# Attention on Trainium2: the softmax reciprocals turned in 32x32 blocks on VectorE and spread over partitions by DMA, with the out-projection two units later

## The chip, the cores and the metric

The kernel runs on one core of one Trainium2 chip. The core has five engines, each with its own queue of instructions that it works through in order: TensorE (PE in the profile, PEld for its weight loads), VectorE (DVE), ScalarE (ACT), GpSimd (POOL) and SyncE (SP), which here only issues transfers. An instruction that waits for a semaphore holds up everything behind it on its own queue. Matrix products write PSUM, which has eight banks of 512 float32 columns on 128 partitions; everything else lives in SBUF (128 partitions) or in device memory, and DMA engines move it between the two.

The metric is the device time in microseconds of one execution, as the median of several runs. A profiled execution is one of its own, so its time stands beside its span.

## The reference

Four layers run one after the other on x of shape 64 x 64 x 256 (64 sequences of 64 tokens), with a conditioning vector of 64 numbers for each sequence. The change lies in the second one:

```python
def _attention(x, W_q, W_k, W_v, W_o):          # 16 heads of 16
    q, k, v = split(x @ W_q.T), split(x @ W_k.T), split(x @ W_v.T)
    attn = softmax(scale * einsum('bnqd,bnkd->bnqk', q, k), axis=-1)
    o = einsum('bnqk,bnkd->bnqd', attn, v)
    return o.transpose(0, 2, 1, 3).reshape(b, l, dm) @ W_o.T

x = x + a_alpha * _attention(_ada_rmsnorm(x, ...), W_q, W_k, W_v, W_o)
return x + f_alpha * _swiglu(_ada_rmsnorm(x, ...), gate_w, hidden_w, out_w, out_b)
```

The first layer is a gated feed-forward network with quantised activations, the third a layer norm, the fourth an adapter whose weights depend on the conditioning.

## The kernel before

The 4096 tokens are worked in 8 blocks of 512 tokens (8 sequences). The first layer runs from 0 to about 258 us, the attention from there to about 445 us, and the feed-forward network of the second layer with the rest from there to the end.

The attention is a loop over 16 units (`for w in range(W)`, line 1070). Unit w is half a block: 4 sequences, 256 tokens. `i, tp = divmod(w, 2)` gives the block and the half; "even" and "odd" units below are tp 0 and 1. Inside a unit the work is split in the steps that the helper functions name:

- `a_score` (649): 64 small products of q and k into four PSUM banks, tag S, of which there is one set.
- `a_shift` (660, 662): for each half of the scores, e = 0 and 1, VectorE takes the maximum of each row and subtracts it; the result is `ex` in SBUF.
- `a_exp` (667, ScalarE) and `a_sum` (671, VectorE): the exponential, and its sum over the keys.
- `a_recip` (676, VectorE): `rz`, the reciprocals of the sums, 32 for each of the 128 partitions. A partition is a query here.
- `a_turn` (690 to 694): 16 transposes on TensorE turn `ex`, so that the keys lie on the partitions; four copies bring them from PSUM to SBUF as `pts`. In odd units two of the four are VectorE's, the other two and all of those of even units ScalarE's.
- `a_weigh` (709): 64 small products of `pts` with the values into one PSUM bank, `po`. Here the partitions are (head, feature), and the columns are queries.
- `a_parts` (725, 726): `of`, the attention's output, is split into a high and a low part, `oh` and `ol`, on ScalarE and POOL. All large products here are three passes over such parts.
- `a_project` (741, 742): the out-projection on TensorE, a product with `at` (from `load_rows`) on VectorE, and an addition on POOL; after odd units the block is stored to memory.

The reciprocals lie on the wrong side for `po`: in `rz` a query is a partition, in `po` it is a column. Before, `a_rows` (681) has ScalarE spread `rz` to `rp`, each reciprocal 16 times side by side, and `a_weigh` turns `rp` with four TensorE transposes (716) into a PSUM bank, copies `po` to SBUF as `of` on ScalarE (713) and multiplies the two on VectorE (717).

The loop is skewed: in unit w the weighing, the parts and the projection of unit w-1 are done. Beside this, each unit does three groups of products for the next block (`todo`: values at lines 83 to 85 through `a_val`, queries and keys through `a_qk`), the norm turns of the block after that (`a_norm_turn`: four TensorE transposes, 259 on VectorE, 260 on POOL, and then its split on ScalarE and POOL), and a splitting of weights for the feed-forward network (`splits.turn`, lines 214 to 219): ScalarE casts (217) a staging tile `st`, POOL subtracts (218), and SP loads the next one (211). There are two staging tiles. One is loaded before the loop; units 1 to 13 call `turn` once, and units 4, 8 and 12 call it twice. The queries, keys and values of the last two units are done, so these hold products of the feed-forward network instead (`f_keep`).

In PSUM, four banks hold S, and four (tag mm) are handed round among `po`, the `todo` products, the norm turns, the out-projection and the transposes of `a_turn`.

What sets the order: the kernel's own text. `tc.manual_schedule(engines=...)` keeps the instructions of the named engines in the order in which the code issues them. In the attention these are TensorE, ScalarE, VectorE and POOL. SP is not named, so its transfers are ordered by the scheduler: `vb` (line 615, the values laid out for the weighing, four transfers per block), `rows` (271), the blocks `ax` (584) and the weight loads (211).

Of the kernel before, what the change touches and what calls it, by code (L numbers as in the profile page):

```python
# [8 lines left out]
F32 = mybir.dt.float32  # L9
# [3 lines left out]
ALU = mybir.AluOpType  # L13
# [4 lines left out]
P = 128  # L18
# [18 lines left out]
def tile_kernel(ctx: ExitStack, tc, xT, x, condT, cw, upT, downT, qkvT, woT, ghT, outT_w,  # L37
# [9 lines left out]
    alphad = dram.tile([3, NB, D], F32, name="alphad")  # L47
    s1d = dram.tile([2, NB, 128, BN], F32, name="s1d")
    s2d = dram.tile([2, NB, 64, D], F32, name="s2d")


    pools = {}
# [9 lines left out]
    def bank(tag):  # L62
        uid[0] += 1
        tags = pools["tags"]
        if tag not in tags:
            tag = "mm"
        return pools["ps"].tile([P, 512], F32, tag=tag, bufs=tags[tag], name=f"{tag}_{uid[0]}")
# [587 lines left out]
    def a_shift(w, e):  # L655

        pool, U = pools["b"], units[w]
        sv = U["pS"][:, 2 * e:2 * e + 2].rearrange("p j (a l) -> p (j a) l", l=L)
        ms = U["mx"][:, 0, 16 * e:16 * e + 16]
        nc.vector.tensor_reduce(ms, sv, AX.X, ALU.max)  # L660
        ex = pool.tile([P, 16, L], F32, tag="ex2", bufs=2, name=f"ex{w}_{e}")
        nc.vector.tensor_tensor(ex, sv, ms.unsqueeze(2).broadcast_to([P, 16, L]), ALU.subtract)
        U["ex"].append(ex)

    def a_exp(w, e):
        ex = units[w]["ex"][e]
        nc.scalar.activation(ex, ex, AF.Exp, scale=0.25)

    def a_sum(w, e):
        pool, U = pools["b"], units[w]  # L670
        nc.vector.tensor_reduce(U["mx"][:, 1, 16 * e:16 * e + 16], U["ex"][e], AX.X, ALU.add)

    def a_recip(w):
        pool, U = pools["b"], units[w]
        rz = U["rz"] = pool.tile([P, 4, 4, 2], F32, tag="rz", bufs=2, name=f"rz{w}")
        nc.vector.reciprocal(rz, U["mx"][:, 1].rearrange("p (j a h) -> p a j h", j=4, h=2))

    def a_rows(w):

        rp = units[w]["rp"] = pools["b"].tile([P, 32, 16], F32, tag="rp", bufs=1, name=f"rp{w}")  # L680
        nc.scalar.copy(rp, units[w]["rz"].rearrange("p a j h -> p (a j h)").unsqueeze(2).broadcast_to([P, 32, 16]))

    def a_turn(w, e):
        U = units[w]
        pv = U["ex"][e].rearrange("p (b h) l -> p b (h l)", h=2)
        pt = pools["b"].tile([P, 2, 512], F32, tag="pts", bufs=2, name=f"pts{w}_{e}")
        for k in range(2):
            pT = bank("mm")
            for a in range(4):
                nc.tensor.transpose(pT[:, a * P:(a + 1) * P], pv[:, 4 * k + a], ident)  # L690
            if w % 2 == 1 and k == 1:
                nc.vector.tensor_copy(pt[:, k], pT)
            else:
                nc.scalar.copy(pt[:, k], pT)
        U["pts"].append(pt)

    def a_weigh(w):

        i, tp = w // 2, w % 2
        pool = pools["b"]  # L700
        U = units.pop(w)
        pts, rp = U["pts"], U["rp"]
        po, vb = bank("po"), ablk[i]["vb"]
        for u in range(2):
            for m in range(2):
                for h in range(2):
                    o = (2 * u + m) * P + h * 64
                    for j in range(4):
                        nc.tensor.matmul(po[32 * j:32 * (j + 1), o:o + 64],
                                         lhsT=vb[:, 2 * tp + u, h, 4 * m + j, :], rhs=pts[j // 2][:, j % 2, o:o + 64],  # L710
                                         start=True, stop=True, tile_position=(0, 32 * j))
        of = pool.tile([P, 512], F32, tag="of", bufs=1, name=f"of{w}")
        nc.scalar.copy(of, po)
        pr = bank("mm")
        for a in range(4):
            nc.tensor.transpose(pr[:, a * P:(a + 1) * P], rp[:, 8 * a:8 * a + 8].rearrange("p h d -> p (h d)"), ident)
        nc.vector.tensor_tensor(of, of, pr, ALU.mult)
        units[w, "f"] = of

    def a_parts(w):  # L720
        pool = pools["b"]
        of = units.pop((w, "f"))
        oh = pool.tile([P, 512], F32R, tag="oh", bufs=3, name=f"oh{w}")
        ol = pool.tile([P, 512], F32R, tag="ol", bufs=3, name=f"ol{w}")
        nc.scalar.copy(oh, of)
        (nc.vector if w == 2 * NBLK - 1 else nc.gpsimd).tensor_tensor(ol, of, oh.bitcast(F32), ALU.subtract)
        units[w, "o"] = (oh, ol)

    def a_project(w):
        i, tp = w // 2, w % 2  # L730
        oh, ol = (o.rearrange("p (u c q) -> p u c q", u=2, c=2) for o in units.pop((w, "o")))
        if tp == 0:
            ablk[i]["x2"] = block(f"ax2_{i}")
        x1, at, x2 = ablk[i]["x1"], ablk[i]["at"], ablk[i]["x2"]
        py = bank("mm")
        for u in range(2):
            for c in range(2):
                mm3(py[:, u * D:(u + 1) * D], (oh[:, u, c], ol[:, u, c]), (wo[0][:, c], wo[1][:, c]),
                    c == 0, c == 1)
        dst = x2[:, 2 * tp:2 * tp + 2]  # L740
        nc.vector.tensor_tensor(dst, py.rearrange("p (t d) -> p t d", d=D), at[:, 2 * tp:2 * tp + 2], ALU.mult)
        nc.gpsimd.tensor_tensor(dst, dst, x1[:, 2 * tp:2 * tp + 2], ALU.add)
        if tp == 1:
            nc.gpsimd.dma_start(out=tok(x2d, i), in_=x2)
            del ablk[i]
# [16 lines left out]
    def f_begin(i):  # L762
        fblk[i]["rs"] = rms(fblk[i]["x2"], f"f{i}")
# [29 lines left out]
    def f_inner(n):  # L793
        pg, pv = f_products(n)
        sg = main.tile([P, T], F32, tag="st", bufs=2, name=f"sg{n}")
        nc.scalar.activation(sg, pg, AF.Silu)  # L796
        if n == LAST:
            return sg, pv
        nc.vector.tensor_tensor(sg, pv, sg, ALU.mult)  # L799
        return sg  # L800
# [263 lines left out]
    def a_norm_turn(i, c):  # L1064
        if i < NBLK:
            return norm_turn(*ablk[i]["n"], i, c, V_AG, V_AB)
        return norm_turn(*fblk[0]["n"], 0, c, V_FG, V_FB)

    late = []
    for w in range(W):  # L1070
        i, tp = divmod(w, 2)
        todo = [lambda k=k: a_ahead(i + 1, k) for k in ((2, 3, 4) if tp == 0 else (5, 6, 7))]
        if i + 1 == NBLK:
            if tp == 0:
                room = rooms()
            todo = [lambda: f_keep(0), lambda: f_keep(1)] if tp == 0 else [lambda: f_keep(2), lambda: a_turn(w, 0)]
            todo.append((lambda: None) if tp == 0 else (lambda: f_silu(0)))
        a_score(w)
        a_shift(w, 0)
        if w > 0:  # L1080
            a_weigh(w - 1)
        a_shift(w, 1)
        if tp == 1:

            if i == 0:
                ablk[0]["at"] = load_rows(0, "alpha", 0)
            if i + 1 < NBLK:
                ablk[i + 1]["at"] = load_rows(0, ("alpha", "ab")[(i + 1) % 2], i + 1)
            if i + 3 < NBLK:
                a_load(i + 3)  # L1090
            elif i + 3 == NBLK:
                f_load(0)
        a_exp(w, 0)
        if w > 0:
            a_parts(w - 1)
        if tp == 0:
            if i + 2 < NBLK:
                a_scale(i + 2)
            elif i + 2 == NBLK:
                f_scale(0)  # L1100
        todo[0]()
        a_sum(w, 0)
        todo[1]()
        a_exp(w, 1)
        todo[2]()
        for rest in late:
            rest()
        late = []
        if tp == 0 and i + 2 <= NBLK:
            late = [a_norm_turn(i + 2, c) for c in range(2)]  # L1110
        a_sum(w, 1)
        if w > 0:
            a_project(w - 1)
        a_recip(w)
        if 1 <= w < 14:
            splits.turn()
            if w % 4 == 0:
                splits.turn()
        if w < W - 1:
            a_turn(w, 0)  # L1120
            a_turn(w, 1)
            a_rows(w)
        if tp == 1:
            if i + 3 < NBLK:
                a_begin(i + 3)
            elif i + 3 == NBLK:
                f_begin(0)
    phase.close()
    pools["ps"] = ctx.enter_context(tc.tile_pool(name="psc", bufs=1, space=PSUM, reuse_waits="tile"))
    pools["tags"] = dict(gh=4, mm=2, acc=2)  # L1130
    a_turn(W - 1, 1)
    a_rows(W - 1)
    s0 = f_kept(0)
    f_parts(0, s0)
    f_silu(1)
    s1 = f_kept(1)
    f_parts(1, s1)
    s3 = f_inner(3)
    a_weigh(W - 1)
    f_silu(2)  # L1140
    s2 = f_kept(2)
    a_parts(W - 1)
    f_outer(0)
    s4 = f_inner(4)
    f_parts(2, s2)
    f_outer(1)
    f_parts(3, s3)
    f_rows(0)
# [139 lines left out]
```

## Time and profile before

| what | value |
|---|---|
| median of 3 runs | 748.91 us (748.66 to 748.92) |
| profiled execution, its own time | 748.95 us |
| its span, first to last instruction | 746.8 us |
| granted TensorE clock | 1.000 |
| attention stage | about 258 to 445 us |
| DMA, mean over the span | 159 GB/s |
| transfers issued by SP in that stage | st, vb, rows, ax |

How to read it: a busy share is the part of the span in which an engine worked. In a group's row stand the line, the engine, the operation, the output and the inputs by their names in the program, and durations in ns as least/median/most. In an engine's timeline the columns are the start in us from the first instruction, the length in us, the engine, the line, the operation and its tiles; xN means that N of them stand merged, and brackets at the end give the idle time before it and who ended it. In a row of DMA issues, the last number is the median time from the issue to the landing. A name such as SPq means the engine's queue: the instruction does no work there, it only issues the transfer.

### The profile page before, as it was taken

What the parts mean: (1) busy time and instruction counts of PE and PEld (TensorE: products, weight loads), DVE (VectorE), ACT (ScalarE), POOL (GpSimd) and SP (SyncE); (2) the same over time, 40 slices, a digit from 0 to 9 for tenths busy, and PEclk for the clock granted to TensorE, in tenths of its full rate; (3) what the DMA queues carried; (4) which work ended last, traced back from release to release, by engine and by line L of the source; (5) the groups of instructions that cost most, each with busy time, mean ns of one, the idle gap of its engine ahead of it and who ended that gap; (6) DMA issues with size and microseconds to landing.
All of it is one profiled execution on the core that took longest, in us unless ns stands there. A gap on an engine that the chain in (4) does not pass through costs nothing.

```text
span 746.8 us, 17456 instructions
## 1 busy us (share of the span) xinstructions
PE 734.7 (98%) x7036; PEld 612.1 (82%) x7036; DVE 542.2 (73%) x843; ACT 405.6 (54%) x849; POOL 340.4 (46%) x359
## 2 busy tenths in 40 slices
PE   9999999999999999999999999999999999999997
PEld 8866766777686878888888888888888888888886
DVE  4998878867687698889888876646555555565676
ACT  5553445335435588998888674535253434434242
POOL 2123133133134426765655427464646464545292
PEclk9999999999999999999999999999999999999999
DMA  8897999999995866444655237623261709080821
GB/s 258 244 265 171 270 280 231 300 278 261 229 273 108 195 153 162 113 134 122 164 150 129 79 101 183 148 52 91 63 163 32 196 4 224 1 198 2 222 62 58
DMA packets 117456, 118.87 MB, mean 159 GB/s; under 512 B 39632, under 2 KB 101200, under 8 KB 117376
## 3 DMA queue, kind: packets, MB, share of 16 engines
q1 hardware_dynamic: 109232, 91.29, 49.6%
q0 software_dynamic: 7488, 25.37, 10.9%
q10 hardware_dynamic: 656, 1.11, 0.5%
q8 instruction: 55, 0.90, 0.5%
q14 instruction: 25, 0.20, 0.1%
HBM read 71.41 MB, written 29.56 MB: 135 GB/s over the span
## 4 chain that ended last, share of the span: by engine, by line
PE 61%; DVE 17%; ACT 11%; issue 5%; DMA 3%; POOL 2%; SPq 1%; DVEq 0%; ACTq 0%; POOLq 0%
PE mm L83 9%; PE mm L85 8%; PE mm L84 8%; PE gh L85 4%; PE gh L84 4%; PE gh L83 4%; PE mm L476 3%; PE mm L298 3%; PE acc L83 2%; DMA wu<-s2d 2%; PE S L649 2%; DVE sg L799 2%; PE acc L85 2%; PE acc L84 2%; ACT x L878 2%
## 5 line engine op out<-in xcount | busy, mean ns | idle before, releaser
L83 PE MATMUL mm<-up,xhl 128*128 128x512 f32 x240 | 97.2, 405 | 0.0
L83 PE MATMUL gh<-xhf,gh 128*128 128x512 f32 x244 | 95.2, 390 | 0.0
L85 PE MATMUL gh<-xhf,gh 128*128 128x512 f32 x244 | 95.2, 390 | 0.0
L84 PE MATMUL gh<-xlf,gh 128*128 128x512 f32 x244 | 95.1, 390 | 0.0
L85 PE MATMUL mm<-up,xll 128*128 128x512 f32 x240 | 93.9, 391 | 0.0
L84 PE MATMUL mm<-up,xhl 128*128 128x512 f32 x240 | 93.6, 390 | 0.0
L799 DVE TENSOR_TENSOR sg<-gh,sg 128x512 f32<-128x512 f32 x60 | 41.3, 688 | 70.7 <-ACT sg L796 37.9
L450 ACT ACTIVATE g<-mm,rs_l 128x512 f32<-128x512 f32 x64 | 43.8, 689 | 80.6 <-PE mm L85 48.1
L837 DVE TENSOR_TENSOR hlo<-sg,hhi 128x512 fp32r<-128x512 f32 x58 | 55.2, 951 | 30.4 <-ACT hhi L836 29.5
L836 ACT CAST hhi<-sg 128x512 fp32r<-128x512 f32 x58 | 36.0, 620 | 71.9 <-DVE sg L799 71.1
L83 PE MATMUL acc<-wout,hhi 128*128 128x256 f32 x248 | 71.9, 290 | 0.0
L85 PE MATMUL acc<-wout,hlo 128*128 128x256 f32 x248 | 69.5, 280 | 0.8 <-DVE hlo L834 0.6
L451 DVE SCALAR_TENSOR_TENSOR h<-mm,rs_l,g 128x512 f32<-128x512 f32 x64 | 46.4, 744 | 32.8 <-PE mm L85 29.7
L84 PE MATMUL acc<-wout,hhi 128*128 128x256 f32 x248 | 69.3, 279 | 0.0
L260 POOL TENSOR_TENSOR xg<-xg,cv 128x512 f32<-128x512 f32 x32 | 35.3, 1114 | 71.2 <-DVE xg L259 71.2
L83 PEld LDWEIGHTS mm<-up,xhl 128*128 128x128 f32 x240 | 45.1, 188 | 15.2 <-issue 2.4
L85 PEld LDWEIGHTS gh<-xhf,gh 128*128 128x128 f32 x244 | 45.8, 188 | 9.6
L85 PEld LDWEIGHTS mm<-up,xll 128*128 128x128 f32 x240 | 45.0, 188 | 10.1
L84 PEld LDWEIGHTS mm<-up,xhl 128*128 128x128 f32 x240 | 45.2, 188 | 8.5
L83 PEld LDWEIGHTS gh<-xhf,gh 128*128 128x128 f32 x244 | 45.8, 188 | 7.3
L84 PEld LDWEIGHTS gh<-xlf,gh 128*128 128x128 f32 x244 | 45.8, 188 | 7.3
L660 DVE TENSOR_REDUCE mx<-S 128x16 f32<-128x1024 f32 x32 | 39.0, 1220 | 17.3 <-PE S L649 17.3
(220 smaller groups left out, 1929.6 us busy)
## 6 DMA issues: line engine op xcount, KB each, us to landing
gt<-in_g SPq DMA_DIRECT2D x32, 512.0 KB, 9.1
rows<-alphad SPq DMA_DIRECT2D x48, 256.0 KB, 4.8
vb<-vx SPq DMA_DIRECT2D x32, 256.0 KB, 5.1
wd<-s1d SPq DMA_DIRECT2D x32, 256.0 KB, 6.2
wu<-s2d SPq DMA_DIRECT2D x32, 256.0 KB, 6.0
xt<-in_x SPq DMA_DIRECT2D x8, 512.0 KB, 7.6
s1d<-stgs POOLq DMA_DIRECT2D x16, 256.0 KB, 8.0
s1d<-stg POOLq DMA_DIRECT2D x16, 256.0 KB, 7.9
```

What stands on the lines that cost most here:

```text
L83: nc.tensor.matmul(out, lhsT=l[0], rhs=r[0], start=first, stop=False)
L84: nc.tensor.matmul(out, lhsT=l[0], rhs=r[1], start=False, stop=False)
L85: nc.tensor.matmul(out, lhsT=l[1], rhs=r[0], start=False, stop=last)
L260: nc.gpsimd.tensor_tensor(b3(xg), b3(xg), bc(vb, c, i), ALU.add)
L298: nc.tensor.matmul(pb[s][c * 64:(c + 1) * 64], lhsT=gl[h], rhs=gt[h, c * GC:(c + 1) * GC], start=True, stop=True, tile_position=(64 * s, 6 ...
L450: nc.scalar.activation(g, pg, AF.Gelu, scale=rs[:, t:t + 1])
L451: nc.vector.scalar_tensor_tensor(h[:, ch * 512:(ch + 1) * 512], pv, rs[:, t:t + 1], g, ALU.mult, ALU.mult)
L476: nc.tensor.matmul(py[:, :D], lhsT=qt[:, f, :], rhs=wq[:, f, :], start=f == 0, stop=f == 7)
L660: nc.vector.tensor_reduce(ms, sv, AX.X, ALU.max)
L799: nc.vector.tensor_tensor(sg, pv, sg, ALU.mult)
L836: nc.scalar.copy(h_hi, sg)
L837: nc.vector.tensor_tensor(h_lo, sg, h_hi.bitcast(F32), ALU.subtract)
```

## The change

`a_rows` now has VectorE turn `rz` in 32x32 blocks: in `zt` a partition 32k+r holds reciprocal r of the queries 32k to 32k+31. Four transfers store the four groups of 32 partitions to a small array in memory, `shares[w]`, which then is 32 rows by 128 queries, and eight transfers load it to `rp`, each row of memory to 16 partitions. `rp` is then 128 partitions by 512 queries in the layout of `po`. `a_weigh` ends with the products; `po` stays in PSUM until `a_parts`, which multiplies it by `rp` on VectorE. All four copies of `a_turn` are ScalarE's in every unit.

The order of the unit changes too. `a_parts(w-1)` moves behind `a_exp(w, 1)`, the first sum and the second group of products; `a_project` comes one unit later, of unit w-2 in unit w, between the two halves of `a_shift`; the two norm turns of an even unit are spread over the even and the odd one; `a_rows(w)` stands before the weight splitting and before `a_turn`. For the whole loop SP is named among the ordered engines, so its transfers are issued in the order of the text as well.

```diff
+    shares = [dram.tile([32, P], F32, name=f"shares{w}") for w in range(2 * NBLK)]
...
     def a_rows(w):
-        rp = units[w]["rp"] = pools["b"].tile([P, 32, 16], F32, tag="rp", bufs=1, name=f"rp{w}")
-        nc.scalar.copy(rp, units[w]["rz"].rearrange("p a j h -> p (a j h)").unsqueeze(2).broadcast_to([P, 32, 16]))
+        zt = pools["b"].tile([P, 32], F32, tag="zt", bufs=1, name=f"zt{w}")
+        nc.vector.transpose(zt, units[w]["rz"].rearrange("p a j h -> p (a j h)"))
+        rp = units[w]["rp"] = pools["b"].tile([P, 4, P], F32, tag="rp", bufs=1, name=f"rp{w}")
+        for k in range(4):
+            nc.sync.dma_start(out=shares[w][:, 32 * k:32 * k + 32], in_=zt[32 * k:32 * k + 32])
+        for n in range(8):
+            nc.sync.dma_start(out=rp[16 * n:16 * n + 16], in_=shares[w].rearrange("(a n) t -> n a t", n=8)[n:n + 1]
+                              .broadcast_to([16, 4, P]))
...
     def a_turn(w, e):
-            if w % 2 == 1 and k == 1:
-                nc.vector.tensor_copy(pt[:, k], pT)
-            else:
-                nc.scalar.copy(pt[:, k], pT)
+            nc.scalar.copy(pt[:, k], pT)
...
     def a_weigh(w):
-        of = pool.tile([P, 512], F32, tag="of", bufs=1, name=f"of{w}")
-        nc.scalar.copy(of, po)
-        pr = bank("mm")
-        for a in range(4):
-            nc.tensor.transpose(pr[:, a * P:(a + 1) * P], rp[:, 8 * a:8 * a + 8].rearrange("p h d -> p (h d)"), ident)
-        nc.vector.tensor_tensor(of, of, pr, ALU.mult)
-        units[w, "f"] = of
+        units[w, "p"] = po, rp

     def a_parts(w):
-        of = units.pop((w, "f"))
+        po, rp = units.pop((w, "p"))
+        of = pool.tile([P, 512], F32, tag="of", bufs=1, name=f"of{w}")
+        nc.vector.tensor_tensor(of, po, rp.rearrange("p a t -> p (a t)"), ALU.mult)
...
+    ordered.close()
+    ordered.enter_context(tc.manual_schedule(engines=engines | {E.SP}))
     for w in range(W):
         a_score(w)
         a_shift(w, 0)
+        if w > 1:
+            a_project(w - 2)
         if w > 0:
             a_weigh(w - 1)
         a_shift(w, 1)
...
         a_exp(w, 0)
-        if w > 0:
-            a_parts(w - 1)
+        todo[0]()
+        a_exp(w, 1)
         if tp == 0:
             if i + 2 < NBLK:
                 a_scale(i + 2)
             elif i + 2 == NBLK:
                 f_scale(0)
-        todo[0]()
+        elif i + 2 <= NBLK:
+            late.append(a_norm_turn(i + 2, 1))
         a_sum(w, 0)
         todo[1]()
-        a_exp(w, 1)
+        if w > 0:
+            a_parts(w - 1)
         todo[2]()
         for rest in late:
             rest()
         late = []
+        a_sum(w, 1)
+        a_recip(w)
+        a_rows(w)
         if tp == 0 and i + 2 <= NBLK:
-            late = [a_norm_turn(i + 2, c) for c in range(2)]
-        a_sum(w, 1)
-        if w > 0:
-            a_project(w - 1)
-        a_recip(w)
+            late = [a_norm_turn(i + 2, 0)]
         if 1 <= w < 14:
             splits.turn()
             if w % 4 == 0:
                 splits.turn()
         if w < W - 1:
             a_turn(w, 0)
             a_turn(w, 1)
-            a_rows(w)
...
+    ordered.close()
+    ordered.enter_context(tc.manual_schedule(engines=engines))
     phase.close()
     a_turn(W - 1, 1)
-    a_rows(W - 1)
...
     s3 = f_inner(3)
+    a_project(W - 2)
     a_weigh(W - 1)
     f_silu(2)
     s2 = f_kept(2)
-    a_parts(W - 1)
     f_outer(0)
     s4 = f_inner(4)
     f_parts(2, s2)
+    a_parts(W - 1)
     f_outer(1)
```

## The prediction

> **What bounds it now.** I read the page's busy shares, the same by 50 us windows, then each engine in order of time in the attention stage (258 to 445 us), and last the DMA rows.
>
> ```profile
> PE 734.7 (98%) x7036; PEld 612.1 (82%) x7036; DVE 542.2 (73%) x843; ACT 405.6 (54%) x849; POOL 340.4 (46%) x359
> ...
> 300.00:350.00 50.00, 49.01 (x907) 42.79 (x906) 44.09 (x52) 45.82 (x100) 34.97 (x33) 1.00 0.50 131
> ```
>
> TensorE (PE, first) binds, but in this window VectorE (44.1 of 50) and ScalarE (45.8) are nearly full as well: a wait of 2 us a unit on either has little slack to vanish in. DMA is half busy. A unit on VectorE (line 717 is `of`, 671 a sum, 676 the reciprocal):
>
> ```profile
> 316.59 0.68 DVE L717 TENSOR_TENSOR of<-of,mm 128x512 f32<-128x512 f32 x1
> ...
> 355.02 1.22 DVE L671 TENSOR_REDUCE mx<-ex 128x16 f32<-128x1024 f32 x1
> 356.16 0.68 DVE L741 TENSOR_TENSOR ax<-mm,rows 128x512 f32<-128x512 f32 x1
> 356.76 0.34 DVE L676 RECIPROCAL rz<-mx 128x32 f32<-128x32 f32 x1
> ```
>
> Start to start, a sum takes 1.14, `of` or an out-projection product 0.60 and a reciprocal 0.26. `of`(0) starts at 272.40 and `of`(14) at 426.91, so 14 units take 154.5 us, 11.04 each.
>
> The work that goes, and the small transfers nearest to those that come:
>
> ```profile
> L716 PE MATMUL mm<-ident,rp x64: 272/273/329, 271.1 to 436.4; 128*128 128x128 f32 x64
> L681 ACT COPY rp<-rz x16: 618/658/694, 269.9 to 434.4; 128x512 f32<-128x512 f32 x16
> ...
> L713 ACT COPY of<-mm x16: 567/586/587, 271.3 to 439.0; 128x512 f32<-128x512 f32 x16
> ```
> ```profile
> 258.62 2.59 SPq L271 DMA_DIRECT2D rows<-alphad  x4
> ...
> 353.78 3.35 SPq L615 DMA_DIRECT2D vb<-vx  x4
> ```
> ```profile
> L211 SPq DMA_DIRECT2D st<-in_ghT x8: 327/340/455, 118.2 to 327.5; - x8
> ```
> ```profile
> out_y<-yo SPq DMA_DIRECT2D x4, 128.0 KB, 1.8
> ```
>
> SP needs 0.65 us per issue for transfers to 64 partitions (2.59 / 4; 0.84 when the queue is loaded), but 0.33 to 0.34 for 128-partition ones. Landing counts from the issue's start.
>
> **The change, part by part.**
> Removed: 64 transposes (a group of four starts at 303.66 and the next product at 304.07: 0.41 a unit, 6.6 us in all), 16 `of` copies and 16 `rp` copies on ScalarE (0.59 and 0.66). ScalarE takes over 16 `pts` copies from VectorE (0.6 each). This gains only where nothing else is later.
>
> Added on VectorE: 16 block transposes of 128x32. No row shows one; bounds are 0.26 (the reciprocal's pitch) and 0.60 (a 512-column product's); I take 0.34, the reciprocal's duration, the same shape.
>
> Added on SP per unit: four stores of 32 rows x 128 bytes, then eight loads to 16 partitions, which wait for all four. 192 issues; 12 x 0.65 = 7.8 us of SP per unit, beside about 6 per two units of its own. From the end of the block transpose: wake 0.1 (my estimate, from the 0.05 us between SP's issues), three pitches 1.95, last store lands 2.2 (1.8 for out_y, plus the 0.3 longer issue; above that up to 3.0, alphad's store), wake 0.1, seven pitches 4.55, last load lands 2.4 (2.0 is the shortest of line 211's, plus 0.3; up to 3.5, the 128 KB weight loads' median): c = 11.3. Pitch 0.65 and not 0.40 (0.34 plus the gap), because few partitions lie nearer to 64 than to 128. Ends: c = 8.0 (0.40, 1.8, 2.0) and 15.1 (0.84, 3.0, 3.5).
>
> The Trainium skill (DMA: Bandwidth & Descriptors, "Issuing engines are not separate DMA queues") calls the sequencer's time to start a DMA "usually small relative to the DMA itself". The row says 0.65 against a landing near 2. By the rule alone the chain would be two landings, about 4.6, hidden, and the sum would be that of the faster rival below.
>
> **The ring.** On VectorE `of`(w) now stands before the second sum of unit w+1, then come reciprocal, block transpose, the chain and `of`(w+1), which waits for all eight loads. Before, `of` waited on products made on TensorE, and no transfer stood between. Round time: 0.60 + 1.14 + 0.26 + 0.34 + 11.3 = 13.64, against 11.04. VectorE's other work in between (two maxima 1.26, two subtractions 1.14, a product 0.60, a sum 1.12: 6.5, at times 0.6 for `xg`, plus the wait for scores) fits inside. So 14 x 13.64 - 154.5 = +36.5. The 6.6 us taken from TensorE are worth nothing there: it waits, because the PSUM bank that the weighing fills stays taken until `of`, and the transposes of `ex` need it.
>
> Start: reciprocal 0 at 268.25, + 0.26 + 0.34 + 11.3 = 280.15 instead of 272.40: +7.75.
>
> **SP in written order.** This is not in the name of the change. Before, SP's order was the scheduler's, and it issued weight loads (line 211) ahead. In units 4, 8 and 12 two staging tiles are split; the casts then follow without a pause:
>
> ```profile
> 311.48 1.16 ACT L217 CAST gh<-st 128x512 fp32r<-128x512 f32 x2
> 312.51 2.08 ACT L694 COPY pts<-mm 128x512 f32<-128x512 f32 x4
> ```
>
> Afterwards the second tile's load is issued behind the eight loads of that unit: 9.55 after the transpose, landing 2.0 to 2.6 later (11.75 on average). ScalarE's cast waits for it, and behind that stand the four `pts` copies, and behind their bank the out-projection, whose VectorE product stands before the next `of`. From landing: cast 0.4, copy 0.5, projection 1.47 (309.55 to 311.02), product 0.60, maximum 1.26, subtraction 1.14, `xg` 0.60, sum 1.12: 18.84 after the transpose instead of 11.3. Three times 7.5: +22.6. At the low ends 5.7 each.
>
> **Tail.** Reciprocal 15 follows `of`(14) after 1.74 instead of 7.03: -5.3. The last out-projection (442.79, 8.85 after that reciprocal) must wait for 0.26 + 0.34 + 11.3 + 0.60 + two casts of 0.6 + 0.1 = 13.8: +4.95.
>
> Priced at nothing: the moved out-projection (same instructions; TensorE, VectorE and POOL have room in a 13.6 us unit), the split of the norm turns (one 0.5 us group a unit), 4.7 MB of traffic (DMA half busy), and the vb, rows and block loads now queued on SP behind the chain: they are needed a unit later. Without that cover the vb issues (3.35) would lengthen the ring of each even unit, at most 7 x 3 us; this lies inside the high end.
>
> Sum: 36.5 + 7.75 + 22.6 - 5.3 + 4.95 = +66.5. The profiled execution took 748.95 (span 746.8, 2.15 around it; the median of the runs is 748.91): 815.
>
> **Rivals.**
> Cheap issues, still slower: with c = 8.0 the ring is 10.3, but in even units `xg` now follows the block transpose, and the second half of the `ex` transposes needs its bank: 2.98 to its end, transposes 1.0, scores 1.2, VectorE 7.12 until the next `of`: 12.3. Seven of 12.3 and seven of 10.3 give +3.4, the start +4.4, three late weight loads +17, tail -3.8: 770 (the tail's -3.8 is -5.3, and +1.5 for the out-projection of unit 14, which now falls into it). For it: TensorE's idle of 0.1 to 0.4 before such transposes today. Against: every 64-partition row costs 0.55 or more.
> Hidden, and faster: transfers of so few bytes are far cheaper than any row shows. VectorE has 6.5 us of work plus 1.4 to 2 of idle after the reciprocal, so from c below 8 the ring costs nothing, and from about 4 the late weight loads shrink to 1 us each. Then TensorE's 6.6 us count, less up to 4 for late loads: 742 to 746. For it: no row has 16 partitions. Against: two landings alone take 3.8.
> No change in effect, with gain and late loads cancelling: 748 to 750, a narrow coincidence.
> Dearer: vb or rows traffic before the stores delays them. c = 15.1 makes the ring 17.4: +89, start +11.6, late loads +24, tail -5.3 + 8.8: 877. For it: the third and fourth vb issue at 355.16 and 356.02 take 0.81 and 1.11 us, so a full queue slows its issuer. Against: at a round of 13.6 us the same traffic is spread over more time.
> The Trainium skill (TensorE: Matmul & The Clock Gate, Part 1) says that TensorE falls to half clock after an idle window of about 3.4 us; here every window was granted 1.00, with gaps under 0.5 us, so nothing shows it. If it came in each late-load gap, an estimate by the page is some 3.4 us each, 10 in all on top.
>
> **Chances and range.** Ring as priced, 790 to 850: 0.70; cheap issues: 0.14; dearer, over 850: 0.10; hidden: 0.04; cancelled: 0.02. The range reaches down to the cheap end and up to 850, 770 to 850, and leaves out 1.6 in 10, the last three. Faster 0.04, within 0.2% (what this kernel's runs can tell) 0.02, slower 0.94.
>
> **What would show it.** Right: VectorE idles some 4 us per unit before `of`, released by a DMA; reciprocals 13 to 14 us apart, three gaps near 21; SP's small issues near 0.6 us; ScalarE idle some 10 us before the second cast of `st` in units 4, 8 and 12; TensorE well under 98% from 280 to 500 us; the later stage unchanged. Wrong: issues of 0.35 or less, or those casts not waiting.

## The result, and the profile after

The changed kernel takes 830.48 us (828.85 to 834.22) where the kernel before takes 748.78: a ratio of 1.1099, 95% interval 1.1062 to 1.1137, slower by 82 us. The forecast was 815 with a range of 770 to 850. The profiled execution took 830.61 us, with a span of 828.8 us.

The first lines are from the page of the changed kernel: the busy shares, and the granted clock in 40 slices of 20.7 us.

```profile
PE 753.0 (91%) x6972; PEld 619.1 (75%) x6972; DVE 539.4 (65%) x843; ACT 399.3 (48%) x833; POOL 340.8 (41%) x359
...
PEclk9999999999999888799799799999999999999999
```

The same 50 us window as before (PE, PEld, DVE, ACT and POOL busy, clock, DMA share, GB/s):

```profile
300.00:350.00 50.00, 36.09 (x529) 30.07 (x527) 26.24 (x29) 23.79 (x47) 19.49 (x18) 0.79 0.44 110
```

Nothing is full any more: TensorE fell from 49.0 to 36.1, VectorE from 44.1 to 26.2, and DMA from 0.50 to 0.44. An attention stage in which every resource idles is bound by waiting. The granted clock falls below 0.9 in slices between 269 and 477 us, which it did nowhere before. From 550 to 800 us TensorE is busy for 248.15 of 250 us, and for 248.23 in the 250 us from 468 before: the later stage is as before.

A unit on VectorE (722 is `of`, 672 a sum, 677 the reciprocal, 682 the block transpose):

```profile
284.18 0.21 DVE L682 STREAM_TRANSPOSE zt<-rz 128x32 f32<-128x32 f32 x1
...
295.79 0.69 DVE L722 TENSOR_TENSOR of<-mm,rp 128x512 f32<-128x512 f32 x1 [1.74 <-DMA rp<-shares]
296.40 1.21 DVE L672 TENSOR_REDUCE mx<-ex 128x16 f32<-128x1024 f32 x1
297.64 0.35 DVE L677 RECIPROCAL rz<-mx 128x32 f32<-128x32 f32 x1
298.03 0.21 DVE L682 STREAM_TRANSPOSE zt<-rz 128x32 f32<-128x32 f32 x1
```

and SP's queue in the same stretch and the next (685 stores, 687 loads; start, length, and how many issues):

```profile
284.42 1.71 SPq L685 DMA_DIRECT2D shares<-zt  x4
290.41 3.60 SPq L687 DMA_DIRECT2D rp<-shares  x8
294.05 0.42 SPq L212 DMA_DIRECT2D st<-in_ghT  x1
...
297.53 1.94 SPq L616 DMA_DIRECT2D vb<-vx  x2
299.57 2.57 SPq L685 DMA_DIRECT2D shares<-zt  x4
305.02 5.67 SPq L687 DMA_DIRECT2D rp<-shares  x8
310.79 0.37 SPq L212 DMA_DIRECT2D st<-in_ghT  x1
```

This is the ring: transpose, four stores, a pause until they have landed (286.13 to 290.41), eight loads, `of`. Behind an odd unit (284.18) `of` starts 11.6 us after the transpose started; behind an even one (298.03, `of` at 312.48) 14.45. Here SP is still issuing `vb` until 299.5, the stores take 2.57 instead of 1.71, and the loads 5.67 instead of 3.60. In the other even units the loads are no slower than in odd ones (3.6 to 4.75 against 3.6 to 5.0); what sets all seven even units with `vb` apart is the time from the end of the transpose to the first load, 6.6 to 9.1 us against 2.9 to 6.0. The ring does not show in every unit: in seven of the sixteen a landing of `rp` is what ends VectorE's idle before `of`, 19.7 us in all.

What the small transfers cost, by the view of the tile `shares` (ns, least/median/most):

```profile
L687 SPq DMA_DIRECT2D rp<-shares x128: 315/426/1727, 276.8 to 516.8; - x128
L685 SPq DMA_DIRECT2D shares<-zt x64: 309/419/1585, 271.2 to 511.5; - x64
```

and, by the view of the tile `zt`, the block transpose:

```profile
L682 DVE STREAM_TRANSPOSE zt<-rz x16: 211/211/213, 267.5 to 510.0; 128x32 f32<-128x32 f32 x16
```

With the gaps between them the pitch is 0.47 us: the eight loads of the first stretch take 3.60 in all. The stores land 3.3 us after issue (median, 1.3 to 5.4), the loads 2.0.

ScalarE in unit 4, where the second weight tile is late:

```profile
327.96 0.61 ACT L218 CAST gh<-st 128x512 fp32r<-128x512 f32 x1
341.16 0.62 ACT L218 CAST gh<-st 128x512 fp32r<-128x512 f32 x1 [12.58 <-DMA st<-in_ghT]
341.69 2.04 ACT L698 COPY pts<-mm 128x512 f32<-128x512 f32 x4
```

and TensorE behind it:

```profile
342.32 0.58 PE L84 MATMUL mm<-wo,oh 128*128 128x256 f32 x1 [10.46 <-ACT pts L698]
342.70 0.41 PE L85 MATMUL mm<-wo,oh 128*128 128x256 f32 x1
342.91 0.41 PE L86 MATMUL mm<-wo,ol 128*128 128x256 f32 x1
```

The cast has waited 12.58 us for a transfer, the copies stand behind it, and TensorE has been idle for 10.46. When it resumes, the out-projection's products follow each other at 0.21 us; elsewhere their pitch is 0.12 (before, 309.77 and 309.89 in unit 4).

From `of`(0) to `of`(14) the changed kernel needs 225.8 us (281.94 to 507.74) against 154.5. The fifteen distances, in order: 13.85, 16.69, 13.08, **24.58**, 11.37, 16.00, 12.36, **24.78**, 11.38, 16.59, 12.82, **26.09**, 12.73, 13.48, 13.63. The bold ones belong to units 4, 8 and 12.

### The profile page after: what moved, and what is told of

It is laid out like the page before. It is cut to its first block, busy times and chain, and to the rows that moved or that the text cites. A ratio compares the mean times of both kernels' runs of the same rounds, so it can differ in the third digit from the quotient of the medians.

```text
span 828.8 us, 17572 instructions
## 1 busy us (share of the span) xinstructions
PE 753.0 (91%) x6972; PEld 619.1 (75%) x6972; DVE 539.4 (65%) x843; ACT 399.3 (48%) x833; POOL 340.8 (41%) x359
## 2 busy tenths in 40 slices
DMA packets 130770, 123.36 MB, mean 149 GB/s; under 512 B 44752, under 2 KB 114512, under 8 KB 130688
## 5 line engine op out<-in xcount | busy, mean ns | idle before, releaser
L261 POOL TENSOR_TENSOR xg<-xg,cv 128x512 f32<-128x512 f32 x32 | 36.1, 1128 | 76.4 <-DVE xg L260 76.3
L84 PE MATMUL mm<-wo,oh 128*128 128x256 f32 x64 | 22.6, 353 | 39.3 <-ACT pts L698 37.8
L697 PE MATMUL mm<-ident,ex 128*128 128x128 f32 x256 | 39.5, 302 | 20.1 <-DVE of L722 10.9
L84 PEld LDWEIGHTS mm<-up,xhl 128*128 128x128 f32 x240 | 45.1, 188 | 15.2 <-issue 2.4
L86 PEld LDWEIGHTS gh<-xhf,gh 128*128 128x128 f32 x244 | 45.8, 188 | 9.7
L86 PEld LDWEIGHTS mm<-up,xll 128*128 128x128 f32 x240 | 45.0, 188 | 10.1
L697 PEld LDWEIGHTS mm<-ident,ex 128*128 128x128 f32 x256 | 31.9, 154 | 26.5 <-DVE of L722 12.0
```

The costliest lines, as they stand in the source:

```text
L84: nc.tensor.matmul(out, lhsT=l[0], rhs=r[0], start=first, stop=False)
L86: nc.tensor.matmul(out, lhsT=l[1], rhs=r[0], start=False, stop=last)
L261: nc.gpsimd.tensor_tensor(b3(xg), b3(xg), bc(vb, c, i), ALU.add)
```

## The experiments

Three explanations were held against each other: the ring of transfers in front of `of`; the late weight loads that SP's written order makes; and anything else (SP as a queue, the lowered clock, the order of the unit on the engines). Unless said otherwise, the kernels differ from the changed one by what the diff shows. Their times stand beside 748.7 to 749.1 us for the kernel before in the same comparison.

**e1: the late weight loads alone.**

```diff
+        if w in (4, 8, 12):
+            splits.load()
         a_score(w)
...
             if w % 4 == 0:
-                splits.turn()
+                splits.turn(load=False)
```

> Units 4, 8 and 12 issue the load of their second weight tile at the start of the unit instead of behind the eight loads of rp; all else as in the changed kernel. If the weight loads in SP's written order cost what the trace suggests, the three long distances from one of to the next (24.6, 24.8 and 26.1 us) fall to the 16 to 16.7 of the other even units, and the distances after them (11.4, 11.4, 12.7) may rise to 13: 830.5 - 26 + 0 to 5 gives 804 to 809 us. If those distances come from the lowered clock or from the banks and not from the loads, they stay above 20 and the time stays within 4 us of 830.5.

Measured: 806.68 us (803.03 to 808.87), ratio 1.0764 (1.0732 to 1.0796), so 23.8 us less. The three long distances became 16.4, 16.1 and 16.1. The late loads are a cause, with their price.

**e2: SP's order left to the scheduler.**

```diff
-    ordered.enter_context(tc.manual_schedule(engines=engines | {E.SP}))
+    ordered.enter_context(tc.manual_schedule(engines=engines))
```

> SP is left to the scheduler in the attention loop, as in the kernel before; the ring of transfers stays. If SP's written order costs only by the late weight loads, they are issued early again and about 22 us go: near 808 us. If the scheduler mixes the rows and vb transfers into the loads of rp, part of that is lost again in longer rings: 808 to 825. If written order costs nothing, 830.

Measured, in one execution: 808.27 us, as with the early loads. What SP's written order cost, as against the scheduler's, is the late loads and hardly anything else.

**e3 and e4: no wait for the loads of `rp`,** without and with the early weight loads.

```diff
-        nc.vector.tensor_tensor(of, po, rp.rearrange("p a t -> p (a t)"), ALU.mult)
+        nc.vector.tensor_tensor(of.rearrange("p (a t) -> p a t", t=P), po.rearrange("p (a t) -> p a t", t=P),
+                                ident.unsqueeze(1).broadcast_to([P, 4, P]), ALU.mult)
```

> of is the product of po with the identity tile, which lies in SBUF from the start, instead of with rp, so the reciprocals are left out of the output; block transposes, stores and loads are all issued as before, and nothing waits for the loads of rp. If the wait in the ring is the cost, the distances from one of to the next become those of the bank path, 10.3 and 12.3 us, but the three late weight loads keep theirs near 24: 748.8 + 3.7 + 3 x 12 + 0 to 5 at the end gives 785 to 794. If the cost lies in SP's issues, in the traffic or in the lowered clock, the time stays above 815. If the late loads were only an effect of the ring, 750 to 757.

> Both edits together: of waits for no transfer, and the second weight tile of units 4, 8 and 12 is loaded at the start of the unit. Output without the reciprocals. If ring and late loads are the whole loss, what is left is the bank path of the new order: 748.8 + 3.7 + 0 to 5 at the end, 750 to 757 us, and a granted clock of 1.00 throughout. If the order of the unit without waits is worth the 6.6 us taken from TensorE, 742 to 746. If a third cause is there (traffic, SP's issues), above 765.

Measured: 821.03 us (one execution), and 791.59 us (789.29 to 792.55), ratio 1.0557 (1.0540 to 1.0575). Both fall where the expectations had put a further cause (above 815, above 765). Taking the wait out of the ring gains 9.5 and 15.1 us, where 36 and 50 at least would have come if ring and late loads were all. So a third thing sets the pace as soon as `of` does not wait. SP's queue in the second of them shows what, over two units:

```profile
362.80 4.26 SPq L688 DMA_DIRECT2D rp<-shares  x8
367.16 0.37 SPq L212 DMA_DIRECT2D st<-in_ghT  x1
367.63 1.26 SPq L273 DMA_DIRECT2D rows<-alphad  x2
369.00 0.55 SPq L586 DMA_DIRECT2D ax<-x1d  x1
369.63 1.85 SPq L686 DMA_DIRECT2D shares<-zt  x4
375.12 3.80 SPq L688 DMA_DIRECT2D rp<-shares  x8
379.02 0.85 SPq L212 DMA_DIRECT2D st<-in_outT_w  x2
380.46 3.36 SPq L617 DMA_DIRECT2D vb<-vx  x4
383.91 3.19 SPq L686 DMA_DIRECT2D shares<-zt  x4
389.11 1.09 SPq L688 DMA_DIRECT2D rp<-shares  x2
```

From 362.80 to 389.11 are 26.3 us, of which 19.5 are issues and most of the rest waits for stores to land: 13.15 us a unit, and from unit 3 to 12 the `of` of this kernel stand 12.9 to 14.6 apart. SP issues the store of the transpose at 367.14 only at 369.63. Among the waits of SP's queue in this kernel from 290 to 445 us there is none of a store for the block transpose, where the changed kernel has these in the same stretch (total, times, longest):

```profile
SPq L685 <- DVE zt L682: 12.1, 4, 4.9
```

So SP runs behind, and what it issues late holds up ScalarE, which works in order: in the same two units ScalarE waits 2.09 us for a weight tile and 1.58 for a block.

**e5, e6, e7: two issues instead of twelve.** With `rz` ordered (j, h, a), the rows of `shares` lie as `rp` reads them, and one store and one load do it. e6 has the early weight loads too; e7 in addition does not wait for `rp`.

```diff
-        for k in range(4):
-            nc.sync.dma_start(out=shares[w][:, 32 * k:32 * k + 32], in_=zt[32 * k:32 * k + 32])
-        for n in range(8):
-            nc.sync.dma_start(out=rp[16 * n:16 * n + 16], in_=shares[w].rearrange("(a n) t -> n a t", n=8)[n:n + 1]
-                              .broadcast_to([16, 4, P]))
+        nc.sync.dma_start(out=shares[w].rearrange("r (k q) -> k r q", k=4), in_=zt)
+        nc.sync.dma_start(out=rp.rearrange("p a t -> p (a t)"),
+                          in_=shares[w].rearrange("(n a) t -> n (a t)", a=4).unsqueeze(1).broadcast_to([8, 16, 4 * P]))
```

> The changed kernel with one store and one load of reciprocals a unit instead of four and eight: the rows of shares are put in the order in which rp reads them, so that each fits one transfer. The chain shrinks by ten issues of 0.465 us to about 0.34 + 3.3 + 0.1 + 2.4 = 6.2 us, below the 8 at which it is hidden under VectorE's work, and the load of the second weight tile is issued 4 us after the block transpose, not 9 to 10. Ring of transfers and late loads: 14 units at 11 to 12.3, three late loads at 2 each, start and tail near nothing: 750 to 765 us. If the store's wait and the granted clock, not the number of issues, carry the loss, more than 785.

> One store and one load a unit, and the second weight tile of units 4, 8 and 12 loaded at the start of the unit. Ring and late loads are both gone: 745 to 757 us, the granted clock back at 1.00. If the order of the unit alone, with no transfer late, costs what was left without the wait (791.6), it stays above 780.

> As the run with one store, one load and early weight loads, and of waits for no transfer (identity in place of rp; the reciprocals are left out of the output). Against the 791.6 us of the same with twelve issues it tells whether SP's queue set the pace there: it had 26.3 us of issues and of waits for stores in two units. If so, 745 to 757, within 4 us of the run with the wait, for which the chain is then hidden. If the order of the unit on the engines set the pace, 785 to 792 again.

Measured: 798.74 us (ratio 1.0665, 1.0647 to 1.0682); 772.07 us (1.0312, 1.0296 to 1.0327); 771.02 us (one execution). The sizes were missed by 14 to 34 us. By its own sign (more than 785) e5 alone would have spoken for the store's wait and the clock; e6 shows that 26.7 us of it are the late loads. Their price had been put at 2 us each, for a load issued 4 us after the transpose. In unit 4 of e5 it is issued 7.75 after the transpose's end (325.42 and 317.67), because the store first waits 3.15 behind `vb`; ScalarE's cast waits 9.59 for it, and three rounds of 23.1 to 23.5 us stay. e6 and e7 lie between their branches, which put a cost of the order alone at 780 and more. Side by side the runs tell the causes apart:

| | twelve issues | two issues |
|---|---|---|
| late weight loads | 830.5 | 798.7 |
| early weight loads | 806.7 | 772.1 |
| early, and `of` does not wait | 791.6 | 771.0 |

With two issues the wait for `rp` is worth about 1 us (e6 against the one execution of e7). Three lines of e6's view of `rp` show why: one issue takes longer than one of the small ones, but ten have gone, and VectorE waits 1.9 us in all.

```profile
L686 SPq DMA_DIRECT2D rp<-shares x16: 596/620/654, 274.4 to 453.7; - x16
...
its engine sat idle before it (us, times) until:
  DMA rp<-shares: 1.9, 3
```

Between e4 and e7 (791.6 and 771.0) no `of` waits for a transfer in either; 20.6 us come from the ten issues and SP's queue alone.

**e8: eight issues more,** on e1: sixteen loads to 8 partitions each.

```diff
-        for n in range(8):
-            nc.sync.dma_start(out=rp[16 * n:16 * n + 16], in_=shares[w].rearrange("(a n) t -> n a t", n=8)[n:n + 1]
-                              .broadcast_to([16, 4, P]))
+        for n in range(16):
+            nc.sync.dma_start(out=rp[8 * n:8 * n + 8], in_=shares[w].rearrange("(a n) t -> n a t", n=8)[n // 2:n // 2 + 1]
+                              .broadcast_to([8, 4, P]))
```

> The kernel with the early weight loads (806.7 us) with sixteen loads to 8 partitions in place of eight to 16: the same bytes in eight more issues a unit. If the issues in the ring set the pace, 14 or 15 rounds grow by 8 x 0.465 = 3.7 us: 858 to 863. If the landing or the clock sets it and the issues overlap with it, less than 825.

Measured, in one execution: 821.46 us, 14.8 more. That is below 825, the sign set for issues that overlap, yet clearly more than nothing. The issues to 8 partitions are shorter than the sum had it:

```profile
L688 SPq DMA_DIRECT2D rp<-shares x256: 263/300/1674, 276.7 to 507.3; - x128
```

Their pitch is 0.345, so the loads grow from 8 x 0.465 = 3.7 to 16 x 0.345 = 5.5 us, 1.8 a unit. The distances behind odd units grew by that or more up to unit 7 (11.4, 12.0 and 12.5 became 14.75, 14.2 and 14.9) and by less later (12.8 and 12.6 became 13.2 and 12.8); those behind even units stayed at 16.0 to 17.4. There SP had issued `vb` further ahead of the transpose, since VectorE came later: its first store starts 0.2 to 0.6 us behind the transpose for units 6, 8 and 12 instead of 1.7 to 2.3.

**e12: `vb` between stores and loads,** on e1. `a_val` puts its four transfers off in the list `behind`.

```diff
         for k in range(4):
             nc.sync.dma_start(out=shares[w][:, 32 * k:32 * k + 32], in_=zt[32 * k:32 * k + 32])
+        while behind:
+            behind.pop()()
         for n in range(8):
```

> The kernel with the early weight loads and twelve issues a unit (806.7 us); in even units the four vb transfers are issued between the stores and the loads of the reciprocals, not ahead of the stores. If they are what makes the even units' chain 14 us instead of 11.4, the distances of 16.2 from one reciprocal to the next fall to about 13.2, seven times: 785 to 789. If the store's landing or the banks make it, the time stays within 4 us of 806.7.

Measured: 802.75 us (800.22 to 805.81), ratio 1.0723 (1.0696 to 1.0749); 4 us less, with an interval that overlaps e1's, so the expected 18 to 22 did not come. The stores now start at once, but SP's queue in an even unit reads

```profile
385.39 1.73 SPq L691 DMA_DIRECT2D shares<-zt  x4
387.22 3.56 SPq L618 DMA_DIRECT2D vb<-vx  x4
390.95 5.71 SPq L695 DMA_DIRECT2D rp<-shares  x8
```

The loads begin 5.8 us after the transpose, and eight of them take 5.7 us; in the even units with `vb` these are 4.6 to 6.3, in the odd ones 3.6 to 5.4. The distances behind even units are 15.3 to 17.2, where e1 has 15.8 to 16.4; the one gain to be seen is the start, where the first store no longer waits 3.6 us for `vb` and `of`(0) comes 1.8 sooner after its transpose. By these rows `vb` costs the ring its issue time and slower issues behind it, of the stores in e1 and of the loads here, and another place in the order hardly changes that. No run left `vb` out.

**e9, e10, e11: what is left in e6.** Two suspects were read from the traces of e6 and e7: ScalarE waits up to 2.5 us for a block, and SP issues in an unlucky order. e9 removes that wait:

```diff
-        ablk[i]["rs"] = rms(ablk[i]["x1"], f"a{i}")
+        ablk[i]["rs"] = rms(ablk[i - 1 if i > 2 else i]["x1"], f"a{i}")
```

e10 leaves it in and makes four moves: the statistics of a block behind the first exponential of the even unit, the block's load ahead of the rows, `vb` behind the store, and the load of `rp` behind the weight load.

```diff
         a_exp(w, 0)
+        if tp == 0 and i > 0:
+            if i + 2 < NBLK:
+                a_begin(i + 2)
...
-            if i + 3 < NBLK:
-                a_begin(i + 3)
...
         nc.sync.dma_start(out=shares[w].rearrange("r (k q) -> k r q", k=4), in_=zt)
+        while behind:
+            behind.pop()()
...
                 splits.turn(load=False)
+        a_spread(w)
```

e11 is e10 with two copies of `pts` per odd unit back on VectorE:

```diff
-            nc.scalar.copy(pt[:, k], pT)
+            if w % 2 == 1 and k == 1:
+                nc.vector.tensor_copy(pt[:, k], pT)
+            else:
+                nc.scalar.copy(pt[:, k], pT)
```

> The kernel with one store, one load and early weight loads (772.1 us), in which the norm statistics of blocks 3 to 7 are taken from the block before, which has long been loaded; so ScalarE does not wait for the load of the new block at the end of the odd units (output changed). In that kernel ScalarE waits there up to 2.2 us for a block whose load SP issues behind the rows, and the exponential, the normalisation and TensorE's transposes of it stand behind. If this is what is left of the loss, 5 units at 2.2 to 3.5 us: 755 to 761. If what is left lies in the order of the unit on the engines themselves, 769 to 773.

> The same kernel (772.1 us) with the computation whole and four moves: the block's load ahead of the rows on SP, its statistics on ScalarE behind the first exponential of the next unit, the store of the reciprocals ahead of the vb transfers, and their load behind the weight load. If late transfers in SP's written order carry what is left, most of the 23 us go: 752 to 762. If not, 768 to 774.

> As the run with the four moves, and the two copies of pts that VectorE made in odd units are VectorE's again. If ScalarE's 16 more copies (0.52 us each, one after another ahead of the out-projection) cost something in this order, 3 to 7 us less than that run. If ScalarE has room, the same within 1 us, or up to 3 slower if VectorE's next maximum comes later.

Measured: 769.18 us (ratio 1.0275, 1.0261 to 1.0289), 769.32 us (1.0275, 1.0254 to 1.0295) and 768.31 us (1.0263, 1.0245 to 1.0282). Each gains 2.8 to 3.8 us over e6, and the copies make no difference that the intervals can tell. e9 alone would not settle it, since its `of` waits 6.8 us for `rp` instead of 1.9; but e10 has the block early as well, and it gains no more. So neither suspect is the rest. The stretch from 258 to 445 us in e7, where `of` waits for no transfer (the first busy time is TensorE's):

```profile
258.00:445.00 187.00, 171.89 (x2812) 140.88 (x2811) 144.53 (x168) 139.75 (x288) 96.02 (x93) 0.97 0.55 137
```

and in the kernel before:

```profile
258.00:445.00 187.00, 183.82 (x3049) 159.64 (x3047) 164.68 (x190) 160.13 (x329) 101.57 (x97) 1.00 0.50 131
```

TensorE idles 8% instead of 2%. In e10 its idle is spread over many small waits between 290 and 430 us, of its weight loads and on ScalarE for the most part. The two largest (total, times, longest):

```profile
PEld mm L258 <- ACT xna L249: 8.2, 20, 1.0
PEld mm L706 <- ACT kb L638: 4.3, 10, 0.6
```

By the reciprocals' starts, e10 needs 171.8 us from the first to the fifteenth where the kernel before needs 154.2: about 1.6 more for each of the five pairs of units in the middle, 3.2 in the first pair, 6.4 in the last, and 5.0 more behind the fifteenth; the first one comes 1.2 sooner. VectorE's waits show where it sits. For scores it waits this long, before from 258 to 445 us and in e10 from 258 to 470:

```profile
DVE mx L660 <- PE S L649: 17.3, 16, 1.9
```
```profile
DVE mx L667 <- PE S L656: 30.3, 16, 3.7
```

In the middle the loss lies behind the even units. From the reciprocal of an even unit to the next one e10 takes 13.4 us, where the kernel before takes 10.5 to 10.9; from an odd one it takes 10.3, where that takes 11.4 to 11.5. Behind unit 8, first before and then in e10:

```profile
358.73 1.22 DVE L660 TENSOR_REDUCE mx<-S 128x16 f32<-128x1024 f32 x1 [1.62 <-PE S L649]
```
```profile
364.04 0.69 DVE L261 TENSOR_TENSOR xg<-mm,cv 128x512 f32<-128x512 f32 x1 [0.25 <-PE mm L258]
367.64 1.22 DVE L667 TENSOR_REDUCE mx<-S 128x16 f32<-128x1024 f32 x1 [2.91 <-PE S L656]
```

A norm turn now stands between the reciprocal and the transposes of `ex`, and the scores come behind both: 4.45 us after the reciprocal (363.19) instead of 1.97. This is read from the trace; no run put the norm turn back. How much is due to it and how much to the later out-projection or the new places of `of` and the sums was not separated, and the losses at both ends stay open. None of these versions comes near the kernel before.

## Why the prediction was right, and where only by luck

The time fell within the range, and the likeliest case, the ring with late weight loads, is the one that came. That the rounds came out at the predicted mean is luck, since their terms were off both ways. Step by step, in its own accounting; the measured end goes by the spans, 828.8 against 746.8:

| step | predicted | measured |
|---|---|---|
| eleven ordinary rounds | 11 x 13.64 = 150.0 | 150.4 |
| three rounds with a late weight load | 3 x 21.2 = 63.5 | 75.45 |
| start | +7.75 | +9.54 |
| behind `of`(14) | -0.35 | +1.2 |

*The ring.* That `of` would wait for twelve issues and two landings, and that the banks behind `po` would stop TensorE, is right, and the mean round, 13.67, is the predicted one. The terms are not. The pitch was 0.47, not 0.65: "few partitions lie nearer to 64 than to 128" was wrong. The stores landed after 3.3 us, not 2.2. The block transpose took 0.211, below its lower bound of 0.26. The sign of some 4 us idle of VectorE per unit before `of` came in part: 24 us in all sixteen units. Odd units that follow no late load had 10.1 to 11.6 from transpose to `of`; even units had 13.8 to 14.45, but unit 14, the only one without `vb`, 11.25. So rounds of about 13.0 and 16.4, and of 11.4 behind a late load, average to what was taken for all. The prediction's term for even units, "priced at nothing" for `vb` behind the chain, is what failed: without that cover it had allowed 7 x 3, and about 3 a unit it was. e12 shows that their place in the order is not what counts; that their issues and traffic are is likely from the rows and from unit 14, but was not tested.

*How much the ring alone is worth.* The prediction counted the whole 36.5 as the wait before `of`. e3 and e4 show that the wait alone is worth 9.5 us with the late loads and 15.1 without; with it gone, SP's queue itself, 26.3 us for two units, is the next bound. Only when the ten issues go as well (e6, e7) do both vanish. The prediction counted SP's 7.8 us per unit and its own 6, but not the time in which SP stands still until the stores have landed: that pause is part of SP's load too.

*Late weight loads.* Place, units and waiting cast are right, and e1 prices them at 23.8 us against 22.6. In the table the rounds are nearly 4 us longer each, as the base of an even unit is 16.4 and not 13.64; the shorter rounds behind them (11.4) give a part back. Unit 4 shows the terms: the load that the cast waits for issued 10.3 after the transpose's end (338.28 and 328.01) instead of 9.55, the cast 2.9 behind that instead of 2.2, and from the cast to `of` 8.98 instead of 7.09, of which 1.5 is the out-projection (342.32 to 345.29, 2.97 instead of 1.47).

*The clock.* "Every window was granted 1.00 … nothing shows it" was true of the trace before (its "gaps under 0.5 us" only of the attention; the longest in the whole trace is 1.0), and the changed trace shows a lower clock: 0.79 in 300 to 350, and 0.96, 0.87 and 0.86 in the three windows of 50 us behind it. Behind the gap of unit 4 it was 0.50 from 342.3 to 345.2 us and 1.00 from 346 to 350. The 1.5 us just named is this. The Trainium skill (TensorE: Matmul & The Clock Gate, Part 1), which the prediction had put aside, has TensorE at half rate until it has been busy for some 4 us, which agrees with the products at 0.21 instead of 0.12 us behind a gap of 10 us. The prediction's estimate of 3.4 us a gap took the whole slow stretch as lost; at half rate half of it is, and here it was 1.5. In the runs the granted mean is higher where TensorE idles less: 0.959 here, 0.971 in e1, 0.990 in e6, 0.994 in e10. What it costs in all was not measured by itself.

*Issue cost against the skill.* The Trainium skill (DMA: Bandwidth & Descriptors, "Issuing engines are not separate DMA queues") calls the time to start a DMA "usually small relative to the DMA itself"; the prediction weighed it against a row of 0.65. The measured value lies between: one issue took 0.43 against a landing of 2.0 to 3.3, but 12 x 0.47 = 5.6 us of issues in an odd unit's chain of 11, and taking ten of them away gained 32 to 35 us.

*Priced at nothing.* The moved out-projection, ScalarE's copies and the split norm turns were to hide. In the changed kernel they lie under the ring, where their price can't be read. But the cheaper rival, which needs a floor, set it at rounds of 12.3 and 10.3; in e7 they are 13.1 to 14.1 and 10.2 to 12.0, and with the ends 22 us remain over the kernel before. In the middle of e10, where `of` waits for no transfer, they are 13.4 to 13.6 and 10.2, so its path through `xg` is there and only too cheap: from `of` to the end of `xg` 3.47 us instead of 2.98 (361.26 to 364.73), to the scores 2.91 instead of 2.2, and from there to the next `of` 7.11, as priced. e5 is that rival in the flesh, a cheap chain with late loads: it took 798.7 where the rival said 770. Two small slips beside: by its own rounds the rival's +3.4 is +3.7, and the added traffic, put at 4.7 MB, was 4.5 (123.36 against 118.87 MB by the pages).

*Start and end.* The first store waited 3.6 us behind the eight `vb` issues of two blocks, which the start's +7.75 did not hold; that and the cheaper pitch leave +9.54. The end is +1.2 instead of -0.35.

## What to carry to other kernels

Count a chain of small transfers by its issues and by the queue that makes them: a wait inside an in-order issuing queue is load on that queue, and what is issued behind it comes late too (in e4 a store by 2.5 us). Before pricing the bytes, ask whether another order at the source makes one transfer of many: here the order of 32 numbers turned twelve issues into two and gave back 32 us. And when a wait is taken out in thought, price the next bound with it, since late loads, ring and queue, and the order of the unit lay over one another here, and each hid the next.

## What the runs showed of the hardware that was not expected

Issue time on SP does not go by partitions alone: 0.30 us for a load to 8 partitions of four pieces each, 0.43 to 16 partitions, 0.62 for one to 128 partitions with a broadcast source, 0.59 for the store of 128 x 32 from 128 partitions, and 0.42 for a quarter of it. Issues of one shape took up to 1.7 us: in the changed kernel the stores of 0.6 us and more stand right behind `vb`'s issues with one exception (484.39), while for the long loads no such rule shows. A store of 4 KB landed after 1.3 to 5.4 us. The block transpose of 128x32 float32 took 0.211 us, less than the 0.35 of a reciprocal of that shape.
